# Global attention with its projection in seven block products, and a planner with other costs

## The chip, the cores and the metric

The kernel runs on one core of a Trainium2 chip, as one launch. The metric is the device time of that launch in microseconds (us). Five engines have instruction streams of their own: PE (matrix products into PSUM), DVE (vector work), ACT (activations and copies), POOL (GpSimd) and SP, which here issues nearly all DMAs. All numbers are f32.

## The reference

x has 8 batches of 512 tokens with 256 channels. The result is three residual steps:

```
x = x + 0.5 * ffn(layernorm(x))
x = x + attn(layernorm(x))
x = x + 0.5 * ffn(layernorm(x))
```

ffn is two layers. Each has local attention with 8 heads of 64 (a shift of half the channels by one token; q, k, v from wqkv; q and k normalized, scaled and rotated; a window of 128 keys back; softmax; the projection wo, 512x256) and a gated unit (layernorm, w1 to 2x682, a * gelu(g), w2 back to 256).

attn is the global part, once per batch. With z = layernorm(x), 16 heads of 16 channels, and W_h the h-th 256x256 block of the weight:

```
s_h = softmax(z_h @ z_h.T / 4)       # z_h: 512x16, s_h: 512x512
out = sum over h of s_h @ (z @ W_h)
```

z @ W_h, a 512x256 matrix times a 256x256 one, is the projection that the change is about: 16 heads x 8 batches = 128 times.

## The kernel before

**A recorded program and a planner.** The code doesn't issue instructions. `Recorder` notes each operation as an `Op`, with dependencies from the regions that it reads and writes (`Plan.touch`); `together()` makes one Op, a group, of several products. `Plan.order` then lists all Ops in one order, from which each engine's stream follows: for every engine it knows when the engine is free and when an Op is ready, and takes, among those that can start within 40 ns of the earliest, the one of lowest rank (the order of recording). Durations come from `Plan.cost`: for each Op a time that it keeps its engine and a time until its result is there. For a DMA, `order` adds a pipe of 170 bytes per ns that all DMAs share. These numbers act on the order alone; on the chip each engine runs its list in order and waits for semaphores. `Plan.issue` (line 369) issues everything, so every row of the profile has the line L369, and operations are told apart by tiles.

**Buffers.** `Pool` and `Ring` hand out SBUF slots and the eight PSUM banks. An SBUF tile that is first written from a bank is reserved with the products that fill that bank (line 281), so such a group is placed when a slot is free.

**Streams.** Two local streams, k = 0 and k = 1, take the even and the odd batches. Each goes through eight blocks (four batches, two passes each) of two layers, `attention` (line 566) and `glu` (line 808), and yields between pieces. The first stream runs six pieces ahead (LAG). After each piece of a stream, one piece of the global stream (line 946) is recorded.

**Local attention.** Per tile t of 128 tokens: `front(t)` makes q, k, v; `scores(t)` multiplies q and k and makes the softmax in tiles `p` (two slots per stream, one for each group g of four heads); `values(t)` multiplies by v; `project(t)` applies wo. In `far` blocks (all but the first and the last) p is turned through DRAM by DMAs (`turned_quarters`, `turned_far`), in the other blocks by transposes on PE. wo is kept for both layers, two tiles of 512 KB, loaded at the start with wqkv (line 393).

**Global heads.** Per batch, z is made and transposed into two tiles zT (`gz`), 128 channels x 512 tokens each. `front(h)` (line 965) loads W_h (`wa`) and the head's 16 rows of zT at four offsets (`hT`), and defines three pieces. `scores` makes four 128x512 products and their exponentials (`e`). `project(half)` (line 988) makes two tiles of 128 tokens in one bank, each from two products (the two halves of the channels, accumulated) with 256 moving columns, and copies the bank to `xw` on DVE. `attend(head, t)` (line 1007) multiplies e by xw, and DVE adds the result into x. While one head attends with t = 0 to 3, the next head's scores and two halves are done after t = 0, 1 and 2.

Of the kernel before, what the change touches and what calls it, by code (L numbers as in the profile page):

```python
# [15 lines left out]
P = 128  # L16
B, N, D = 8, 512, 256
NT = N // P
# [158 lines left out]
class Plan:  # L177
# [55 lines left out]
    def cost(self, op):  # L233

        if op.engine == "tensor":

            lanes, op.mode = {}, "whole"
            for name, args, kw in op.calls:
                lane, t = 0, 109.0
                if name == "matmul":  # L240
                    a = kw["lhsT"]
                    lane, t = (a.region()[0], args[0].region()[0]), 2 * max(0.842 * elements(kw["rhs"]), 0.852 * a.shape[1])
                    k, m = a.shape
                    op.mode = "fours" if k <= 32 else "quarters" if k <= 64 and m <= 64 else "halves" if k <= 64 else "columns" if m <= 64 else "whole"
                lanes[lane] = lanes.get(lane, 0.0) + t
            busy = max(lanes.values())
            return busy, busy + 170
        name, args, kw = op.calls[0]
        n = max(elements(a) for a in (*args, *kw.values()) if hasattr(a, "shape"))
        if name == "dma_start":  # L250
            return 580.0, 2300.0
        if op.engine == "scalar":
            if name == "activation":
                op.mode = {AF.Exp: "exp", AF.Gelu: "gelu"}.get(args[2])
                busy = 70 + 0.82 * n + (105 if "bias" in kw else 0)
                return (busy + 93, busy + 310) if "accum_out" in kw else (busy, busy + 110)
            return 70 + 0.81 * n, 175 + 0.81 * n
        if op.engine == "vector":
            if name == "tensor_tensor_reduce":
                return 90.0 + n, 250.0 + n  # L260
            if name == "bn_stats":
                return 70.0 + n, 150.0 + n
            return 90 + 1.035 * n, 170 + 1.035 * n
        if name == "memset":
            return 80 + 0.85 * n, 100 + 0.85 * n
        if ALU.pow in args:
            return 350.0 + 157 * n, 400.0 + 157 * n
        return 210 + 1.98 * n, 250 + 1.98 * n

    def order(self):  # L270

# [18 lines left out]
        pipe = 0.0  # L290
# [17 lines left out]
        while len(order) < len(self.ops):  # L308
# [30 lines left out]
            op.end = op.start + op.done  # L339
            if op.calls[0][0] == "dma_start":  # L340
                a = op.calls[0][2]["out"]
                pipe = max(pipe, op.start + 2000.0) + elements(a) * a.shape[0] * 4 / 170
                op.end = pipe + 300
            for x in op.opens:
                _, x.slot = x.ring.free.pop(0)
                x.ring.open(x.stream, x.turn)
# [29 lines left out]
def macaron(ctx: ExitStack, tc: tile.TileContext, x, weight, wqkv, wo, w1, w2, b2, vecs, qk_scales, rotary, out):  # L376
# [16 lines left out]
    def load_attention(l):  # L393

        wq = wpool.tile([P, 2, 3 * INNER], F32, tag=f"wqkv{l}", name=f"wqkv{l}")
        for part in range(3):
            cols = slice(part * INNER, (part + 1) * INNER)
            nc.sync.dma_start(out=wq[:, :, cols], in_=wqkv[l, :, cols].rearrange("(k p) f -> p k f", p=P))
        o = wpool.tile([P, NPAIR, D], F32, tag=f"wo{l}", name=f"wo{l}")
        nc.sync.dma_start(out=o, in_=wo[l].rearrange("(k p) f -> p k f", p=P))  # L400
        return wq, o

    def load_glu(l):

# [18 lines left out]
    load_x(0)  # L423
    load_x(1)
    attention_weights = [load_attention(0)]
    glu_weights = [load_glu(0)]
    attention_weights.append(load_attention(1))
    tabs, vec = [], []
# [137 lines left out]
    def attention(k, y, l, far):  # L566
        wqkv_sb, wo_sb = attention_weights[l]
# [4 lines left out]
        v = {}  # L572

        kT = work.tile([P, NPAIR, 2, P], F32, tag=f"kT{k}", bufs=1)

# [54 lines left out]
        def scores(t, pair, rn):  # L630
# [21 lines left out]
            for g in range(2):  # L652
# [16 lines left out]
                with plan.together():  # L669
                    for i in range(2):  # L670
                        keys = kT[:, 2 * g + i].rearrange("p j k -> p (j k)")
                        for q, to, ks in sorted(pieces, key=lambda piece: piece[1].start - piece[1].stop):
                            for par in range(2):
                                rows = slice(par * DH, (par + 1) * DH)
                                nc.tensor.matmul(
                                    sps[par][q, i, to], lhsT=qT[rows, 2 * g + i, q], rhs=keys[rows, ks], start=True, stop=True
                                )
                heads = slice(4 * g, 4 * g + 4)

                if far:  # L680
# [51 lines left out]
        def values(t, probs):  # L732
# [63 lines left out]
        for t in range(NT):  # L796
# [128 lines left out]
    def stream(k, blocks):  # L925

        for n, (b, second) in enumerate(blocks):
            while second and (b, True) not in done:
                next(others, None)
            y = layernorm(xs[b], k)  # L930
            yield
            for l in range(DEPTH):
                step = DEPTH * n + l
                far = FAR and 0 < n < len(blocks) - 1
                yield from attention(k, y, l, far)
                yield from glu(k, y, step, xs[b], far)

                if k == 1 and step + 1 < DEPTH * len(blocks):
                    glu_weights.append(load_glu((step + 1) % DEPTH))
                if l == 0 and n + 1 < len(blocks) and blocks[n + 1][0] not in xs:  # L940
                    load_x(blocks[n + 1][0])
            done.add((b, False))
            if second:
                nc.sync.dma_start(out=out[b].rearrange("(t p) c -> p t c", p=P), in_=xs[b])

    def global_heads(b):
# [13 lines left out]
            zT.append(z)  # L960

        def front(h):

            w = work.tile([P, 2, D], F32, tag="wa", bufs=2)
            nc.sync.dma_start(out=w, in_=weight[h * D : (h + 1) * D, :].rearrange("(c p) f -> p c f", p=P))

            hT = work.tile([P, N], F32, tag="hT", bufs=2)  # L970
# [4 lines left out]
            es, xw = [], []  # L975

            def scores():
                sps = [bank([P, N]) for s in range(NT)]
# [4 lines left out]
                for s in range(NT):  # L983
                    e = work.tile([P, N], F32, tag="e", bufs=2 * NT)
                    nc.scalar.activation(e, sps[s], AF.Exp, scale=1.0 / AHD**0.5, accum_out=rsum[:, s : s + 1])
                    es.append(e)

            def project(half):
                pv = bank([P, 2, D])
                with plan.together():  # L990
                    for i in range(2):
                        s = 2 * half + i
                        for c in range(2):
                            nc.tensor.matmul(
                                pv[:, i, :],
                                lhsT=zT[c][:, s * P : (s + 1) * P],
                                rhs=w[:, c, :],
                                start=(c == 0),
                                stop=(c == 1),
                            )  # L1000
                xv = work.tile([P, 2, D], F32, tag="xw", bufs=4)
                nc.vector.tensor_copy(xv, pv)
                xw.append(xv)

            return es, xw, rsum, (scores, lambda: project(0), lambda: project(1))

        def attend(head, t):
            es, xw, rinv, _ = head
            pa = bank([P, D])
            with plan.together():  # L1010
                for s in range(NT):
                    nc.tensor.matmul(
                        pa, lhsT=es[s][:, t * P : (t + 1) * P], rhs=xw[s // 2][:, s % 2, :], start=(s == 0), stop=(s == NT - 1)
                    )
            xt = xs[b][:, t, :]
            nc.vector.scalar_tensor_tensor(xt, pa, rinv[:, t : t + 1], xt, ALU.mult, ALU.add)
# [122 lines left out]
```

## Time and profile before

| | us |
|---|---|
| time, median of 3 runs (3947.79 to 3949.27) | 3949.23 |
| the profiled execution's own time | 3952.0 |
| its span, first to last instruction | 3950.1 |
| PE busy (98% of the span) | 3878.5 |
| PE busy with projection records (work_wa, work_gz), 2048 of them | 477.6 |
| DVE busy (62%) | 2447.9 |
| ACT busy (45%) | 1766.9 |
| POOL busy (31%) | 1233.7 |

A row of a group reads: line, engine, operation, written tile <- read tiles, form (rows x elements), count | busy us, mean ns of one | idle us of the engine before it, and what ended that. In a product's form `128*128 128x256` the first pair is the weights' rows and columns, the second the rows and moving columns. PEld is the loading of weights, which the trace records apart from PE's moving. One f32 product is two records of each. The ends of PE's records are modelled and overlap the next start, so distances from start to start are the safer measure. The granted clock of PE was 0.994 over the whole span.

### The profile page before, as it was taken

To read this page: it belongs to the slowest core of one execution; us is meant where nothing else is said; L and a number is where in the kernel's file an instruction comes from. 1 tells how busy PE (TensorE), PEld (TensorE's weight loads), DVE (VectorE), ACT (ScalarE), POOL (GpSimd) and SP (SyncE) were. 2 spreads that over 40 slices of the span, in tenths; PEclk is the share of its full clock that TensorE was granted. 3 is DMA by queue.
4 is the path that set the end of the run, shared out by engine and by line. 5 is a ranking of instruction groups with operands and counts; after the bars stand their busy time and mean duration, and the time that the engine had idled before them with its cause. 6 is when DMAs were issued, how large, how long until landed. Compare 5 with 4: busy or idle time off the path is not lost.

```text
span 3950.1 us, 72878 instructions
## 1 busy us (share of the span) xinstructions
PE 3878.5 (98%) x26240; PEld 2659.5 (67%) x26240; DVE 2447.9 (62%) x6888; ACT 1766.9 (45%) x4548; POOL 1233.7 (31%) x1132
## 2 busy tenths in 40 slices
PE   8999999999999999999999999999999999999998
PEld 4566776766767667677676776767767667686665
DVE  7676655667566665674765747657466565535674
ACT  5565534535344353452443534535335353324564
POOL 6242323424133341341422405324133242103240
PEclk9999999999999999999999999999999999999999
DMA  3000543534435344253442534525335244110000
GB/s 116 1 24 27 155 135 104 150 98 140 129 104 153 93 128 143 88 165 92 128 138 94 155 104 130 159 91 156 91 116 157 81 143 134 61 33 9 1 24 11
DMA packets 437644, 400.74 MB, mean 101 GB/s; under 512 B 53954, under 2 KB 379172, under 8 KB 437284
## 3 DMA queue, kind: packets, MB, share of 16 engines
q1 hardware_dynamic: 436420, 394.76, 33.5%
q8 instruction: 208, 3.41, 0.4%
q10 hardware_dynamic: 864, 1.33, 0.1%
q14 instruction: 152, 1.25, 0.1%
HBM read 235.49 MB, written 143.66 MB: 96 GB/s over the span
## 4 chain that ended last, share of the span: by engine, by line
PE 81%; DVE 5%; issue 2%; ACT 2%; POOL 1%; DMA 0%; SPq 0%; DVEq 0%; POOLq 0%; ACTq 0%
PE psum_bank L369 81%; ACT work_p L369 2%; DVE work_p L369 2%; DVE work_qn L369 1%; DVE small_ss L369 1%; POOL small_rn L369 0%; POOL work_t L369 0%; ACT work_both L369 0%; DVE work_xw L369 0%; DVE small_bnst L369 0%; SPq L369 0%; DVE work_both L369 0%; DVE work_o L369 0%; DVE xpool_x L369 0%; POOL small_rstd L369 0%
## 5 line engine op out<-in xcount | busy, mean ns | idle before, releaser
L369 PE MATMUL psum_bank<-work_xw,work_e 128*128 128x256 f32 x4096 | 960.0, 385 | 3.0 <-ACT work_e L369 1.9
L369 PEld LDWEIGHTS psum_bank<-work_xw,work_e 128*128 128x128 f32 x4096 | 765.8, 191 | 199.0 <-issue 47.2
L369 PE MATMUL psum_bank<-wpool_wqkv,zpool_z 128*128 128x512 f32 x1536 | 712.2, 603 | 2.7 <-ACT work_v L369 2.0
L369 ACT ACTIVATE work_p<-work_p,small_nmax,small_rn 128x192 f32<-128x192 f32 (+2 forms) x1024 | 543.7, 533 | 324.2 <-DVE small_nmax L369 213.7
L369 POOL TENSOR_TENSOR work_t<-work_qn,const_tab 128x256 f32<-128x256 f32 x512 | 397.4, 797 | 590.3 <-ACT work_qn L369 503.5
L369 PE MATMUL psum_bank<-zpool_z,wpool_w 128*128 128x512 f32 x1280 | 558.9, 595 | 1.5 <-DVE zpool_z L369 1.5
L369 POOL TENSOR_TENSOR small_rn<-small_ss,const_nhalf 128x8 f32<-128x8 f32 x256 | 484.4, 1893 | 149.8 <-DVE small_ss L369 141.6
L369 POOL TENSOR_TENSOR work_p<-work_p,small_ri 128x768 f32<-128x768 f32 (+1 forms) x192 | 264.4, 1378 | 778.9 <-DVE small_ri L369 371.9
L369 ACT ACTIVATE work_e<-psum_bank 128x512 f32<-128x512 f32 x512 | 298.3, 596 | 420.4 <-PE psum_bank L369 403.9
L369 PE MATMUL psum_bank<-work_wa,work_gz 128*128 128x256 f32 x2048 | 477.6, 381 | 5.9 <-DVE work_gz L369 3.9
L369 PEld LDWEIGHTS psum_bank<-wpool_wqkv,zpool_z 128*128 128x128 f32 x1536 | 284.8, 192 | 288.1 <-issue 266.4
L369 PEld LDWEIGHTS psum_bank<-zpool_z,wpool_w 128*128 128x128 f32 x1280 | 243.5, 191 | 301.8 <-issue 273.7
L369 PEld LDWEIGHTS psum_bank<-work_wa,work_gz 128*128 128x128 f32 x2048 | 385.3, 190 | 78.3 <-issue 14.7
L369 DVE SCALAR_TENSOR_TENSOR xpool_x<-psum_bank,gsmall_rinv,xpool_x 128x256 f32<-128x256 f32 x512 | 242.2, 474 | 283.6 <-PE psum_bank L369 281.2
L369 ACT COPY work_qn<-psum_bank 128x512 f32<-128x512 f32 x256 | 148.4, 582 | 327.1 <-PE psum_bank L369 263.8
L369 DVE SCALAR_TENSOR_TENSOR work_p<-psum_bank,const_vec,work_p 128x512 f32<-128x512 f32 x128 | 95.7, 749 | 278.1 <-PE psum_bank L369 226.9
L369 PE MATMUL psum_bank<-wpool_wo,work_o 128*128 128x256 f32 x1024 | 244.9, 383 | 6.4 <-DVE work_o L369 6.2
L369 PE MATMUL psum_bank<-wpool_w,work_p 128*128 128x256 f32 x1024 | 243.2, 380 | 0.0
L369 DVE COPY work_xw<-psum_bank 128x512 f32<-128x512 f32 x256 | 173.8, 680 | 108.4 <-PE psum_bank L369 107.9
L369 DVE TENSOR_REDUCE small_ss<-work_sq 128x8 f32<-128x512 f32 x256 | 172.2, 673 | 109.0 <-ACT work_sq L369 108.1
L369 PEld LDWEIGHTS psum_bank<-wpool_wo,work_o 128*128 128x128 f32 x1024 | 191.4, 190 | 56.7 <-DVE work_o L369 16.1
L369 ACT ACTIVATE work_p<-psum_bank,const_vec 128x512 f32<-128x512 f32 x128 | 87.9, 687 | 296.6 <-PE psum_bank L369 288.0
(89 smaller groups left out, 4943.3 us busy)
## 6 DMA issues: line engine op xcount, KB each, us to landing
work_p<-dram_quarters SPq DMA_DIRECT2D x576, 128.0 KB
dram_quarters<-work_p SPq DMA_DIRECT2D x288, 192.0 KB
dram_turned<-work_both SPq DMA_DIRECT2D x96, 512.0 KB
work_both<-dram_turned SPq DMA_DIRECT2D x384, 128.0 KB
work_wa<-in_weight_dram SPq DMA_DIRECT2D x128, 256.0 KB
wpool_w<-in_w_dram SPq DMA_DIRECT2D x48, 640.0 KB
work_hT<-work_gz SPq DMA_DIRECT2D x512, 32.0 KB
dram_turned<-work_p SPq DMA_DIRECT2D x48, 256.0 KB
```

The lines of the kernel that those rows point to most:

```text
L369: getattr(getattr(nc, op.engine), name)(*map(real, args), **{k: real(a) for k, a in kw.items()})
```

## The change

It has four parts.

**The projection.** z is split into four blocks of 256 tokens x 128 channels (a11, a12, a21, a22, views of zT), W_h into four of 128x128 (b11 to b22). POOL makes four sums of the a's once per batch (tile `sums`) and four differences of the b's per head, three instructions. Seven products of blocks take the place of eight: each is two products on PE with 128 moving columns, one per tile of tokens. They lie in four groups, with a bank each: a11 b11; a12 b21 and s2 t2; s3 t3 and s1 t1; a22 t4 and s4 b22. An ACT copy (`u1`) and four additions on DVE put the blocks of the result together in `xw`, in place of two copies. `attend` reads the same elements of xw, in another layout. hT has one buffer in place of two.

**wo per layer.** One tile, loaded at the start and then again for every layer step, recorded where the second stream ends its attention (15 more times).

**The planner's numbers.** DMAs, ACT, DVE and POOL get other constants, with terms for PSUM sources and for operands that are single values per partition; the shared DMA pipe is 330 bytes per ns in place of 170; SP isn't given a further DMA while eight are under way by the plan.

**Scores behind the last values.** In far blocks the score groups of a tile t > 0 get a dependency on both value groups of the tile before.

```diff
         if name == "dma_start":
-            return 580.0, 2300.0
+            source = kw["in_"]
+            far = isinstance(source, View) and source.tile.ring.space == DRAM
+            return (560.0 if len(source.shape) > 3 and far else 450.0), 2400.0 if far else 1900.0
         if op.engine == "scalar":
+            base = 60 if args[1].tile.ring.space == PSUM else 100
...
-                busy = 70 + 0.82 * n + (105 if "bias" in kw else 0)
-                return (busy + 93, busy + 310) if "accum_out" in kw else (busy, busy + 110)
-            return 70 + 0.81 * n, 175 + 0.81 * n
+                busy = base + 0.82 * n + (105 if "bias" in kw else 0)
+                return (busy + 92, busy + 280) if "accum_out" in kw else (busy, busy + 105)
+            return base + 0.81 * n, base + 105 + 0.81 * n
         if op.engine == "vector":
...
-            return 90 + 1.035 * n, 170 + 1.035 * n
+            pointers = sum(isinstance(u, View) and elements(u) == 1 for u in args[1:])
+            busy = 70 + 1.035 * n + (55 if pointers and name == "scalar_tensor_tensor" else 27 * pointers)
+            return busy, busy + 85
...
         if ALU.pow in args:
-            return 350.0 + 157 * n, 400.0 + 157 * n
-        return 210 + 1.98 * n, 250 + 1.98 * n
+            return 248.0 * n - 10, 248.0 * n + 30
+        busy = 140 + (2.14 if n <= 2 * P else 1.67) * n
+        return busy, busy + 45
...
-                pipe = max(pipe, op.start + 2000.0) + elements(a) * a.shape[0] * 4 / 170
-                op.end = pipe + 300
+                pipe = max(pipe, op.start + op.done - 400) + elements(a) * a.shape[0] * 4 / 330
+                op.end = pipe + 400
+                flying = sorted(flying + [op.end])[-8:]
+                if len(flying) == 8:
+                    free[e] = max(free[e], flying[0])
...
+                if far and t > 0:
+                    plan.ops[-1].after.update(latest)
...
+                    latest[g:] = [plan.ops[-1]]
...
+        if k == 1 and step + 1 < 2 * DEPTH * B // 2:
+            output_weights.append(load_wo((step + 1) % DEPTH))
...
+        a11, a12, a21, a22 = (zT[c][:, r * N // 2 : (r + 1) * N // 2] for r in range(2) for c in range(2))
+        sums = work.tile([P, 4, N // 2], F32, tag="sums")
+        for i, (u, v, op) in enumerate(
+            ((a21, a22, ALU.add), (sums[:, 0], a11, ALU.subtract), (a11, a21, ALU.subtract), (a12, sums[:, 1], ALU.subtract))
+        ):
+            nc.gpsimd.tensor_tensor(sums[:, i], u, v, op)
+        s1, s2, s3, s4 = (sums[:, i] for i in range(4))
...
+            nc.gpsimd.tensor_tensor(diffs[:, :2], blocks[:, 1::2], blocks[:, :2], ALU.subtract)
+            t1, t3, t2, t4 = (diffs[:, i] for i in range(4))
+            nc.gpsimd.tensor_tensor(t2, b22, t1, ALU.subtract)
+            nc.gpsimd.tensor_tensor(t4, b21, t2, ALU.subtract)
...
+            def product(*pairs):
+                ps = bank([P, len(pairs), 2, P])
+                with plan.together():
+                    for i, (left, right) in enumerate(pairs):
+                        for t in range(2):
+                            nc.tensor.matmul(ps[:, i, t, :], lhsT=left[:, t * P : (t + 1) * P], rhs=right, start=True, stop=True)
+                return ps.rearrange("p i t f -> p i (t f)")
+
             def project(half):
-                pv = bank([P, 2, D])
-                with plan.together():
-                    for i in range(2):
-                        s = 2 * half + i
-                        for c in range(2):
-                            nc.tensor.matmul(
-                                pv[:, i, :], lhsT=zT[c][:, s * P : (s + 1) * P], rhs=w[:, c, :], start=(c == 0), stop=(c == 1),
-                            )
-                xv = work.tile([P, 2, D], F32, tag="xw", bufs=4)
-                nc.vector.tensor_copy(xv, pv)
-                xw.append(xv)
+                spread = lambda u: u.unsqueeze(1).to_broadcast([P, 2, N // 2])
+                pairs = whole.rearrange("p (a b) m -> p b a m", b=2)
+                if half == 0:
+                    p1 = product((a11, b11))
+                    u1 = work.tile([P, N // 2], F32, tag="u1")
+                    nc.scalar.copy(u1, p1[:, 0])
+                    nc.vector.tensor_add(pairs[:, 0], product((a12, b21), (s2, t2)), spread(u1))
+                    return
+                ps = product((s3, t3), (s1, t1))
+                nc.vector.tensor_add(pairs[:, 1], ps, spread(whole[:, 2]))
+                nc.vector.tensor_add(whole[:, 2], ps[:, 1], whole[:, 1])
+                nc.vector.tensor_add(pairs[:, 1], product((a22, t4), (s4, b22)), pairs[:, 1])
```

`whole` is `xw` as four blocks of 256 columns, each two token tiles of 128 channels.

More of the change, by code (lines that the diff above doesn't have):

```diff
@@ L250, in cost @@
         if name == "dma_start":
-            return 580.0, 2300.0
+            source = kw["in_"]
+            far = isinstance(source, View) and source.tile.ring.space == DRAM
+            return (560.0 if len(source.shape) > 3 and far else 450.0), 2400.0 if far else 1900.0
         if op.engine == "scalar":
+            base = 60 if args[1].tile.ring.space == PSUM else 100
             if name == "activation":
                 op.mode = {AF.Exp: "exp", AF.Gelu: "gelu"}.get(args[2])
-                busy = 70 + 0.82 * n + (105 if "bias" in kw else 0)
-                return (busy + 93, busy + 310) if "accum_out" in kw else (busy, busy + 110)
-            return 70 + 0.81 * n, 175 + 0.81 * n
+                busy = base + 0.82 * n + (105 if "bias" in kw else 0)
+                return (busy + 92, busy + 280) if "accum_out" in kw else (busy, busy + 105)
+            return base + 0.81 * n, base + 105 + 0.81 * n
         if op.engine == "vector":
             if name == "tensor_tensor_reduce":
-                return 90.0 + n, 250.0 + n
+                return 86.0 + n, 190.0 + n
             if name == "bn_stats":
-                return 70.0 + n, 150.0 + n
-            return 90 + 1.035 * n, 170 + 1.035 * n
+                return 60.0 + n, 145.0 + n
+            pointers = sum(isinstance(u, View) and elements(u) == 1 for u in args[1:])
+            busy = 70 + 1.035 * n + (55 if pointers and name == "scalar_tensor_tensor" else 27 * pointers)
+            return busy, busy + 85
         if name == "memset":
@@ L289, in order @@
         free, mode = dict.fromkeys(self.ENGINES, 0.0), dict.fromkeys(self.ENGINES)
-        pipe = 0.0
+        pipe, flying = 0.0, []
         candidates = {e: [op for op in self.ops if op.engine == e and not op.waits] for e in self.ENGINES}
@@ L398, in load_attention, with load_wo @@
             nc.sync.dma_start(out=wq[:, :, cols], in_=wqkv[l, :, cols].rearrange("(k p) f -> p k f", p=P))
-        o = wpool.tile([P, NPAIR, D], F32, tag=f"wo{l}", name=f"wo{l}")
+        return wq
+    def load_wo(l):
+        o = wpool.tile([P, NPAIR, D], F32, tag="wo")
         nc.sync.dma_start(out=o, in_=wo[l].rearrange("(k p) f -> p k f", p=P))
-        return wq, o
+        return o
     def load_glu(l):
@@ L425, in macaron @@
     attention_weights = [load_attention(0)]
+    output_weights = [load_wo(0)]
     glu_weights = [load_glu(0)]
@@ L564, in later, with attention @@
         return later_of[k]
-    def attention(k, y, l, far):
-        wqkv_sb, wo_sb = attention_weights[l]
+    def attention(k, y, step, far):
+        l = step % DEPTH
+        wqkv_sb, wo_sb = attention_weights[l], output_weights[step]
         z0 = zpool.tile([P, N + 1], F32, tag=f"z{k}", bufs=2)
@@ L571, in attention @@
         z1 = shifted(tiled, k)
-        v = {}
+        v, latest = {}, []
         kT = work.tile([P, NPAIR, 2, P], F32, tag=f"kT{k}", bufs=1)
@@ L934, in stream @@
                 far = FAR and 0 < n < len(blocks) - 1
-                yield from attention(k, y, l, far)
+                yield from attention(k, y, step, far)
                 yield from glu(k, y, step, xs[b], far)
@@ L960, in global_heads @@
             zT.append(z)
-        def front(h):
-            w = work.tile([P, 2, D], F32, tag="wa", bufs=2)
-            nc.sync.dma_start(out=w, in_=weight[h * D : (h + 1) * D, :].rearrange("(c p) f -> p c f", p=P))
-            hT = work.tile([P, N], F32, tag="hT", bufs=2)
+        a11, a12, a21, a22 = (zT[c][:, r * N // 2 : (r + 1) * N // 2] for r in range(2) for c in range(2))
[5 more added lines that the diff above has]
+        s1, s2, s3, s4 = (sums[:, i] for i in range(4))
+        def front(h):
+            w = work.tile([P, 2, 4, P], F32, tag="wa", bufs=2)
+            blocks, diffs = w[:, 0], w[:, 1]
+            nc.sync.dma_start(
+                out=blocks.rearrange("p (c f) q -> p c (f q)", c=2),
+                in_=weight[h * D : (h + 1) * D, :].rearrange("(c p) f -> p c f", p=P),
+            )
+            b11, b12, b21, b22 = (blocks[:, i] for i in range(4))
+            nc.gpsimd.tensor_tensor(diffs[:, :2], blocks[:, 1::2], blocks[:, :2], ALU.subtract)
+            t1, t3, t2, t4 = (diffs[:, i] for i in range(4))
+            nc.gpsimd.tensor_tensor(t2, b22, t1, ALU.subtract)
+            nc.gpsimd.tensor_tensor(t4, b21, t2, ALU.subtract)
+            hT = work.tile([P, N], F32, tag="hT", bufs=1)
             at = h % (P // AHD) * AHD
@@ L974, in front @@
             rsum = gsmall.tile([P, NT], F32, tag="rsum")
-            es, xw = [], []
+            es = []
+            xw = work.tile([P, 4, 2, P], F32, tag="xw", bufs=2)
+            whole = xw.rearrange("p i t f -> p i (t f)")
             def scores():
@@ L986, in scores @@
                     es.append(e)
-            def project(half):
-                pv = bank([P, 2, D])
-                with plan.together():
-                    for i in range(2):
-                        s = 2 * half + i
-                        for c in range(2):
-                            nc.tensor.matmul(
[L995 to L999, printed above, removed]
-                            )
-                xv = work.tile([P, 2, D], F32, tag="xw", bufs=4)
-                nc.vector.tensor_copy(xv, pv)
-                xw.append(xv)
+            def product(*pairs):
[5 more added lines that the diff above has]
+                return ps.rearrange("p i t f -> p i (t f)")
+            def project(half):
+                spread = lambda u: u.unsqueeze(1).to_broadcast([P, 2, N // 2])
[10 more added lines that the diff above has]
+                nc.vector.tensor_add(pairs[:, 1], product((a22, t4), (s4, b22)), pairs[:, 1])
             return es, xw, rsum, (scores, lambda: project(0), lambda: project(1))
@@ L1012, in attend @@
                     nc.tensor.matmul(
-                        pa, lhsT=es[s][:, t * P : (t + 1) * P], rhs=xw[s // 2][:, s % 2, :], start=(s == 0), stop=(s == NT - 1)
+                        pa.rearrange("p (i f) -> p i f", i=2),
+                        lhsT=es[s][:, t * P : (t + 1) * P],
+                        rhs=xw[:, (slice(0, 4, 3), slice(1, 3))[s // 2], s % 2, :],
+                        start=(s == 0),
+                        stop=(s == NT - 1),
                     )
```

## The prediction

> **What bounds the kernel now.** I read the page's busy shares and slices first, then the busy times of stretches, then PE's timeline, then the groups of the other engines. From the page:
>
> ```profile
> span 3950.1 us, 72878 instructions
> ...
> PE 3878.5 (98%) x26240; PEld 2659.5 (67%) x26240; DVE 2447.9 (62%) x6888; ACT 1766.9 (45%) x4548; POOL 1233.7 (31%) x1132
> ...
> PE   8999999999999999999999999999999999999998
> ```
>
> Busy times by stretch (length; busy time and instructions of each engine; granted clock; DMA share; GB/s):
>
> ```profile
> 0.00:100.00 100.00, 80.40 (x632) 47.84 (x633) 79.03 (x225) 56.65 (x147) 63.32 (x73) 1.00 0.34 115
> 100.00:300.00 200.00, 189.67 (x1510) 119.97 (x1509) 137.18 (x396) 117.55 (x281) 66.39 (x64) 0.98 0.04 12
> 300.00:3300.00 3000.00, 2985.89 (x20089) 2063.33 (x20088) 1883.34 (x5314) 1312.52 (x3459) 976.03 (x873) 1.00 0.41 122
> 3300.00:3600.00 300.00, 298.07 (x1585) 222.15 (x1584) 126.78 (x323) 83.81 (x231) 28.72 (x28) 1.00 0.19 55
> 3800.00:3950.00 150.00, 131.84 (x994) 84.17 (x992) 86.09 (x250) 77.98 (x169) 29.12 (x27) 0.94 0.02 8
> ```
>
> From 300 to 3600 us, where the global heads run beside the local layers, PE idles 16 of 3300 us. The other 56 us of its 71.6 us of idle lie at the two ends, without heads. In the middle all other work fills in behind PE: a microsecond taken off PE's queue there is a microsecond off the end, and work added to DVE, ACT or POOL costs nothing until PE waits for it.
>
> **Seven products (project).** Before, a head has 8 products with 256 moving columns; the trace has 2048 records for 128 x 8 = 1024 calls, so two records per product, each with its weight load. After, it has 14 products with 128 moving columns: 28 records of 128x128. No such f32 product is in the trace, so its price is bounded. PE's timeline:
>
> ```profile
> 355.23 1.89 PE L369 MATMUL psum_bank<-work_wa,work_gz 128*128 128x256 f32 x8
> 356.96 0.82 PE L369 MATMUL psum_bank<-const_ident,work_p 128*128 128x128 f32 x6
> 357.62 1.89 PE L369 MATMUL psum_bank<-work_wa,work_gz 128*128 128x256 f32 x8
> 359.35 3.60 PE L369 MATMUL psum_bank<-zpool_z,wpool_w 128*128 128x512 f32 x8
> ```
>
> Ends are modelled, so I go from start to start: 8 records of 256 columns take 1.73 us (216 ns each), 6 transposes with 128 columns and 128x128 weights of their own 0.66 us (110 ns each). The danger is the weight load: its record lasts 190 ns (page, mean), and if it couldn't run ahead, 28 x 0.190 = 5.32 us would replace 2 x 1.73 = 3.46 us. So 110 ns below, 190 ns above. Two rows of f32 products that are not transposes decide, in another window:
>
> ```profile
> 2004.27 0.31 PEld L369 LDWEIGHTS psum_bank<-work_hT 16*128 16x128 f32 x8 [0.33 <-issue]
> ...
> 2009.54 0.90 PE L369 MATMUL psum_bank<-work_p,work_v 64*64 64x128 f32 x32
> ...
> 2010.37 1.99 PE L369 MATMUL psum_bank<-work_xw,work_e 128*128 128x256 f32 x8
> ```
>
> Eight loads of 128 columns, two on each of four sets of 16 rows, end within 0.31 us although each lasts 0.18: the second follows the first by at most 0.13 us. And the 32 records of values are eight rounds of four at a time, 128 and 64 columns in turn, each with a load of 64 columns. At 110/128 = 0.86 ns per column moving takes 4 x 192 x 0.86 = 0.66 us, the loads 8 x 55 = 0.44 us; one after the other would be 1.10 us, and the group took 0.83. Loads as long as what they hide behind are hidden. I take 110 ns: 28 x 0.110 = 3.08 us per head, 0.38 us less, **-49 us** over 128 heads.
>
> [...]
>
> **Twice as many groups.** Two groups of products per head become four, each with its own bank, so 256 more entries. An entry is free in the rows above (1.73 us for 8 both times) and costs about 0.09 us where work of another kind comes next (from 2002.45, where eight of the same records start, to 2004.27 is 1.82 us). Bounds 0 and 256 x 0.09 = 23 us. Entries between neighbouring products are near the free row; I take a quarter, **+6 us**.
>
> **DVE, ACT and POOL.** Prices of the added operations, from groups by form:
>
> ```profile
> L369 DVE COPY work_xw<-psum_bank 128x512 f32<-128x512 f32 x256 | 173.8, 680 | 108.4 <-PE psum_bank L369 107.9
> ...
> L369 DVE TENSOR_TENSOR work_o<-psum_bank,work_o 128x512 f32<-128x512 f32 x96 | 65.6, 683 | 24.4 <-ACT work_o L369 23.8
> ...
> L369 ACT COPY work_both<-psum_bank 128x256 f32<-128x256 f32 x32 | 10.6, 369 | 10.6 <-PE psum_bank L369 10.6
> L369 DVE TENSOR_TENSOR work_o<-psum_bank,work_o 128x256 f32<-128x256 f32 x32 | 13.3, 416 | 1.5 <-ACT work_o L369 1.5
> ...
> L369 POOL TENSOR_TENSOR const_tab<-const_tab,zpool_z 128x256 f32<-128x256 f32 x8 | 5.7, 741 | 3.2 <-DMA zpool_z<-in_qk_scales_dram 3.2
> ```
>
> DVE: two copies of 680 ns go, three additions of 683 and one of 416 come: 2465 - 1360 = +1.1 us per head, 141 us; it rises from 63% to 67% in the middle. ACT: one copy of 369, 47 us, 45% to 46%. POOL: per head one subtraction of 256 columns (741 ns) and two of 128, which the trace lacks (between half of 741 and 741; I take 500): 1.74 us, 223 us, and four of 741 per batch, 24 us: about 250 us, 31% to 38%. All lies under PE's 2986 of 3000 us and I cost it at nothing; bare, DVE's part would be 141 us. One piece can show. The last half was one copy behind the last product. Now the third group needs 0.68 + 0.42 = 1.1 us of DVE while the fourth occupies PE for 8 x 0.110 = 0.88, so the last addition starts 0.22 us late, on every head 28 us. PE already waits here:
>
> ```profile
> PEld psum_bank L369 <- DVE work_xw L369: 26.2, 35, 1.3
> ```
>
> 35 waits for 256 copies, 14%; as PE mostly has other work in between, I charge about that share, **+3 us**.
>
> [...]
>
> **wo per layer.** 16 loads of 512 KB in place of 2, 7 MB more beside 401 MB; 14 more issues of 0.37 us on SP. With one buffer a load waits for the second stream's last projection and has to land by the first stream's next one. Between these the trace has some 70 us (groups at 603 and 674, 345 and 421 us), and 512 KB at the 122 GB/s of the middle are 4 us: 0. On SP the load stands ahead of the round trips through DRAM of both streams; planned behind the projection it waits for, it holds them only if PE lags the plan. The single buffer of hT likewise gets a head's length (11.6 us at the least: 160 records in ten heads from 3480 to 3596 us) for four loads of 32 KB: 0.
>
> **Planner and scores.** New costs and at most eight DMAs in flight move every engine's order, without altering a single instruction; scores of a later tile of a far block now stand behind both value groups of the tile before, whose p buffers they mostly need anyway. No row prices an order. Below: all of PE's idle time, -71 us. Above: PE idling in the middle as it does from 100 to 300 us (5.2% in place of 0.5%), 3300 x 4.7% = +155 us. I take 0, as the middle's 16 us are nearer to nothing left to gain and the filling work hasn't shrunk.
>
> **Sum.** -49 + 6 + 3 = -40 us. The profiled execution took 3952.0 us (span 3950.1 and 1.9 around it), 2.8 over the median of 3949.2; it becomes 3912, the median **3909 us**, -1.0%.
>
> **Rivals.** *The new order also fills the ends* (chance 0.12): half of the 56 us of idle at the ends goes with the 40: 3880. For it: the ends have gaps that a truer model can see. Against: they lie where streams wait for their own chain. *Entries and waits eat the gain* (0.06): 23 us of entries and 15 us of waits for xw in place of 6 and 3 leave -11 us, and a few more none: 3945. *The new order starves PE* (0.12, the slower one): the planner now lets DMAs land earlier (330 bytes per ns in place of 170), so DVE, ACT and POOL queues can stand behind a tile of p still under way, and PE behind them. It decides from 40 us: PE idle in the middle at 0.5 + 40/3300 = 1.7%. At 2.5%, +66 us, it gives 3975. For it: SP already waits in order; against: heads are ready to fill nearly any gap. I count loads that don't hide within this 0.12. That the products don't fall in time at all is this last case.
>
> **How the numbers follow.** The forecast holds 0.70, with its own range 3885 to 3935 (entries and waits at their ends, the order at +-15). A measurement tells 0.2%, 8 us, from no change. Faster: 0.70 + 0.12 = 0.82; same 0.06; slower 0.12. The range runs from 3872, where the first rival is nearly covered, to 3946, which leaves out the slower case.
>
> **What would show it.** 3584 records of 128x128 for work_gz, 110 ns from start to start; PE busy near 3840 us; ten heads in the lone stretch near the end in 112 us in place of 116; DVE near 2590 us, POOL near 1485. Wrong would be: starts 124 ns apart or more, PE idle over 1.7% in the middle, or weight loads waiting for xw well over 26 us.

## The result

The changed kernel takes **4067.6 us** (median of 5 runs, 4062.6 to 4081.3), against 3949.2 us before: **1.0308 times as long, 95% interval 1.0288 to 1.0328**, 118 us more. Forecast were 3909 us, with a range from 3872 to 3946.

### The profile page after: what moved, and what is told of

Same layout as the page of the kernel before. It is cut to its first block, busy times and chain, and to the rows that moved or that the text cites. A ratio compares the mean times of both kernels' runs of the same rounds, so it can differ in the third digit from the quotient of the medians.

```text
span 4070.3 us, 77051 instructions
## 1 busy us (share of the span) xinstructions
PE 3902.9 (96%) x27776; PEld 2740.7 (67%) x27776; DVE 2583.0 (63%) x7144; ACT 1821.5 (45%) x4690; POOL 1464.4 (36%) x1548
## 5 line engine op out<-in xcount | busy, mean ns | idle before, releaser
L381 PE MATMUL psum_bank<-work_xw,work_e 128*128 128x256 f32 x4096 | 981.0, 388 | 21.4 <-DVE work_xw L381 10.0
L381 POOL TENSOR_TENSOR work_t<-work_qn,const_tab 128x256 f32<-128x256 f32 x512 | 386.9, 776 | 507.6 <-ACT work_qn L381 501.1
L381 POOL TENSOR_TENSOR work_wa<-work_wa 128x128 f32<-128x128 f32 (+1 forms) x384 | 220.4, 576 | 721.8 <-DMA work_wa<-in_weight_dram 576.0
L381 PE MATMUL psum_bank<-work_wa,work_sums 128*128 128x128 f32 x2048 | 294.5, 277 | 3.7 <-POOL work_sums L381 2.9
L381 PEld LDWEIGHTS psum_bank<-work_wa,work_sums 128*128 128x128 f32 x2048 | 269.4, 193 | 18.2 <-issue 4.8
L381 DVE TENSOR_TENSOR work_xw<-psum_bank,work_xw 128x512 f32<-128x512 f32 (+1 forms) x384 | 228.2, 594 | 55.0 <-PE psum_bank L381 45.5
```

The costliest lines, as they stand in the source:

```text
L381: getattr(getattr(nc, op.engine), name)(*map(real, args), **{k: real(a) for k, a in kw.items()})
```

## The profile after

The page of the changed kernel: span, busy shares, and PE by slices.

```profile
span 4070.3 us, 77051 instructions
...
PE 3902.9 (96%) x27776; PEld 2740.7 (67%) x27776; DVE 2583.0 (63%) x7144; ACT 1821.5 (45%) x4690; POOL 1464.4 (36%) x1548
...
PE   8999999999999999999999999999999999999998
```

Its busy times by stretch, with the same columns as before:

```profile
100.00:300.00 200.00, 186.69 (x1512) 119.69 (x1505) 134.65 (x396) 120.76 (x285) 66.19 (x62) 0.98 0.05 15
300.00:3300.00 3000.00, 2907.57 (x20522) 2056.64 (x20521) 1924.86 (x5319) 1320.06 (x3429) 1116.84 (x1179) 0.98 0.40 120
```

DVE and POOL came out as forecast (2590 and 1485 us). What is new is PE's idle time, 167 us in place of 72, and of the 96 us more, 78 lie in the middle stretch (92 of 3000 us in place of 14). PE's busy time didn't fall to 3840; it rose by 24, and the granted clock of the middle stretch is 0.98 where it was 1.00. The slices hide this: 97% is still a 9.

Who PE waited for, the longest and two more (us in total, times, longest):

```profile
PE psum_bank L381 <- DMA work_p<-dram_quarters: 44.1, 47, 2.6
...
PE psum_bank L381 <- DVE work_xw L381: 12.8, 16, 1.8
...
PE psum_bank L381 <- DMA work_p<-dram_turned: 2.6, 3, 1.9
```

Before, PE waited for no DMA of p at all, and 1.4 us in all for xw (`PE psum_bank L369 <- DVE work_xw L369: 1.4, 3, 0.7`). Now it stops 47 times at a value group whose p is still on its way back from DRAM. One of these stops in PE's timeline (start, length from first start to last end):

```profile
2074.24 1.05 PE L381 MATMUL psum_bank<-work_wa,work_sums 128*128 128x128 f32 x8
2075.14 0.61 PE L381 MATMUL psum_bank<-work_wa,work_gz 128*128 128x128 f32 x4
...
2079.19 1.11 PE L381 MATMUL psum_bank<-work_p,work_v 64*64 64x128 f32 x36
2082.94 1.54 PE L381 MATMUL psum_bank<-work_p,work_v 64*64 64x128 f32 x28 [2.65 <-DMA work_p<-dram_quarters]
2084.41 3.78 PE L381 MATMUL psum_bank<-work_xw,work_e 128*128 128x256 f32 x8
2087.99 2.39 PE L381 MATMUL psum_bank<-wpool_wo,work_o 128*128 128x256 f32 x8
```

Two things are to be seen. The forecast price of the new products holds: 8 records of 128 columns take 0.90 us (2074.24 to 2075.14), 112 ns each. And after the 2.65 us of waiting, the next 8 records of 256 columns take 3.58 us (2084.41 to 2087.99), 447 ns each in place of 216. The busy times around this place, with the granted clock as the third number from the end, say why:

```profile
2068.00:2082.00 14.00, 12.29 (x110) 10.40 (x108) 11.90 (x35) 3.17 (x10) 3.10 (x3) 1.00 0.63 188
2082.20:2089.00 6.80, 6.06 (x39) 5.08 (x40) 1.18 (x2) 1.35 (x3) 1.63 (x3) 0.50 0.69 229
2089.00:2103.00 14.00, 14.00 (x56) 8.46 (x55) 4.58 (x11) 5.45 (x12) 0.00 (x0) 1.00 0.16 43
```

This wait cost twice: its own length of 2.65 us, and then time at half clock. The clock falls 1.9 us after PE ran out of work and stays at half for 6.8 us, of which PE works 6.1. Not every wait does this: the middle stretch of this trace has 39 stops of PE of over 0.9 us, and at 21 of them such a dip begins during the stop or within 4 us behind it. Over the span the mean clock is

```profile
core 0: 4070.3 us, clock 0.982
```

```profile
core 0: 3950.1 us, clock 0.994
```

after and before. Added up from the records of the clock, 145 us of 4070 are at half speed in place of 46 of 3950; less the 11.5 and 4.0 us in which PE stood still anyway, 133 and 42 us are left, and half the difference, by this estimate about 46 us, is lost (447 ns a record above in place of 216). That the stops bring the dips is read from where they lie in time. Over the runs below, half-speed time grows with PE's idle time, but not in step: 56 us with 118 idle in before_latency, 104 with 137 in before_newcosts.

## The experiments

All compare with the kernel before, run again beside them on the same chip (medians 3946 to 3947 us); proj_wo, the projection with only what it needs in memory, serves as a base for others. Each diff shows what the label changes in its base.

### Which part loses: proj_wo, before_newcosts, after_olddma, before_signal

proj_wo is the change without the planner's numbers and without the dependency of scores. (wo per layer and the single buffer of hT stay with it.)

```diff
-            return (560.0 if len(source.shape) > 3 and far else 450.0), 2400.0 if far else 1900.0
+            return 580.0, 2300.0
...
-                pipe = max(pipe, op.start + op.done - 400) + elements(a) * a.shape[0] * 4 / 330
-                op.end = pipe + 400
+                pipe = max(pipe, op.start + 2000.0) + elements(a) * a.shape[0] * 4 / 170
+                op.end = pipe + 300
```

after_olddma is the changed kernel with just these lines taken back and the limit in flight left out; proj_wo takes back the other costs and the dependency too. before_newcosts puts all new numbers into the kernel before. before_signal has `SIGNAL = 112.0` in place of 110, the planner's allowance for a semaphore: the same work in a slightly other order.

> The kernel before with the seven-product projection and wo per layer, but the planner's old numbers and no dependency of scores on the last values. Theory A (the new DMA numbers make the order too early, PE then waits for the quarters of p): 3905 to 3930 us, PE waits for DMA work_p<-dram_quarters under 5 us. Theory B (the projection's own work on DVE, POOL and the banks starves PE whatever the order): 4030 to 4080 us.

> The kernel before with only the planner's new numbers (all engines, the DMA pipe and the limit of eight in flight). Theory A: 4000 to 4080 us, with PE waiting 40 us or more for DMA work_p<-dram_quarters. Theory B: within 15 us of the kernel before, 3935 to 3965 us.

> The changed kernel with only the DMA numbers of the planner put back (580 and 2300 ns, a pipe of 170 bytes per ns, no limit in flight); ACT, DVE and POOL keep the new ones. Theory A: 3905 to 3935 us, PE hardly waits for DMAs. Theory B: 4040 to 4080 us. If the new numbers of the engines are to blame and not those of the DMAs: 4000 to 4070 us.

> The kernel before with the planner's allowance for a semaphore at 112 ns in place of 110: the same work, another order. It measures what any new order moves by itself. Theories A and B: within 10 us of 3949. Theory C (every order but the one found is worse by chance): 3980 us or more.

| run | us | ratio, 95% interval |
|---|---|---|
| proj_wo | 3965.0 | 1.0045 (1.0030 to 1.0059) |
| before_newcosts | 4040.5 | 1.0231 (1.0214 to 1.0248) |
| after_olddma | 3965.5 | 1.0047 (1.0032 to 1.0062) |
| before_signal | 3948.9 | 1.0004 (0.9995 to 1.0012) |

The planner's numbers, which change no instruction, lose 94 us by themselves, and the DMA numbers are 102 of the 118 us. Theory A holds in its first half: the DMA numbers lose the time. But no theory foresaw 3965 us for proj_wo and after_olddma, where A asked for 3930 or 3935 at most: the projection gains nothing without the new numbers; it loses 18 us.

### The DMA numbers: before_latency, after_p90

before_latency has the new landing times and pipe, without a limit in flight and with the old costs of the engines. after_p90 is the changed kernel with later landings alone:

```diff
-            return (560.0 if len(source.shape) > 3 and far else 450.0), 2400.0 if far else 1900.0
+            return (560.0 if len(source.shape) > 3 and far else 450.0), 3900.0 if far else 2900.0
```

> The kernel before with the planner's new DMA latencies and the pipe of 330 bytes per ns, but no limit of eight in flight; costs of ACT, DVE and POOL old. Theory A1 (the plan takes transfers to be there too early): 4020 to 4050 us, PE waits 40 us or more for DMA work_p<-dram_quarters. Theory A2 (the limit in flight moves the DMAs' order, and that is what costs): within 10 us of the kernel before.

> The changed kernel with only the planner's time to a DMA's landing raised, from 2400 and 1900 ns to 3900 and 2900, near the late tenth of the landings that other engines waited for in the changed kernel's trace; the pipe of 330 bytes per ns and all else stay. Theory A (planned landings at the middle of the trace are too early for engines that run in order): 3955 to 3985 us, as with the old DMA numbers. If only the slow pipe of 170 helps, as it spaces transfers out: 4030 to 4060 us.

before_latency: 3999.1 us, 1.0129 (1.0113 to 1.0145). after_p90: **3959.9 us**, 1.0026 (1.0015 to 1.0038), 108 us below the changed kernel. The wait for the quarters of p, in before_latency and then in after_p90:

```profile
PE psum_bank L371 <- DMA work_p<-dram_quarters: 29.8, 38, 2.2
```

```profile
PE psum_bank L381 <- DMA work_p<-dram_quarters: 2.5, 6, 0.8
```

So the cause is when the plan takes a transfer to have landed: put later, it ends the loss, though the pipe stays fast. before_latency and before_p90 (below), which differ in the landing times alone and have no limit in flight, are 44 us apart in the same way; before_latency itself falls short of the 4020 us and the 40 us of waiting that theory A1 asked for. In the change, though, the constant for a read back from DRAM didn't get shorter: with its surcharge it rose from 2300 to 2400 ns. What brought the landings forward was the pipe, 0.40 us for 128 KB in place of 0.77, with hardly a queue behind it. Worked out with each kernel's own planner, the 576 reads of quarters are planned to land this long after their issue:

| planner of | middle, us | ninetieth percentile, us |
|---|---|---|
| before | 4.6 | 7.6 |
| the changed kernel | 2.8 | 2.8 |
| after_p90 | 4.3 | 4.3 |

In the changed kernel's trace, the reads of quarters that some engine waited for landed 2.96 us after their issue in the middle and 3.9 us at the ninetieth percentile (77 of them; those that nobody waited for leave no time). 60 of the 77 landed later than the planned 2.8 us, 4 later than 4.3. A value group needs the last of several transfers, and PE takes its list in order (the attend products of 2084.41 above stood behind the stop, though every xw written before them was there by 2080.63), so there was no slack for the late ones. The old pipe of 170 bytes per ns is slower than what the chip moved in the stretch above (229 GB/s), so it was wrong, and it left slack. No run changes the pipe's rate alone.

### The engines' numbers and the dependency: before_engines, after_nobehind

before_engines has the new costs of ACT, DVE and POOL with the DMA lines old; after_nobehind is

```diff
-                if far and t > 0:
-                    plan.ops[-1].after.update(latest)
```

> The kernel before with the planner's new numbers for ACT, DVE and POOL alone, the DMA numbers old. With the DMA latencies alone it took 3999 us, with all new numbers 4040. If the engines' numbers cost by themselves: 3985 to 3995 us. If they cost only where the plan has no slack left for the DMAs: 3942 to 3956 us.

> The changed kernel without the dependency of scores on the last values. If that dependency costs nothing, as forecast: 4055 to 4080 us. If it holds PE's freedom to fill gaps and so is part of the loss: 4020 to 4045 us. If it shortens the waits for the quarters, and without it they grow: 4085 us or more.

before_engines: 3972.7 us, 1.0068 (1.0053 to 1.0083): between the two expectations, PE idle 88 us in place of 72. With them and the limit in flight, the DMA numbers make 4040 in place of 3999 (before_newcosts against before_latency); no run has the limit alone, which by the planner holds SP back 32 times in before_newcosts. On top of the seven products the engines' numbers and the dependency cost nothing that shows (after_olddma against proj_wo). Why they cost here isn't settled. after_nobehind: 4060.0 us, 1.0286 (1.0270 to 1.0303), so the dependency costs at most some 8 us and is no part of the story.

### Why the projection doesn't gain: before_wo_hT, proj_nodiff, proj_copies

before_wo_hT is the kernel before with wo per layer and `hT` at `bufs=1`. The other two are proj_wo with part of the work left out:

```diff
-            nc.gpsimd.tensor_tensor(diffs[:, :2], blocks[:, 1::2], blocks[:, :2], ALU.subtract)
-            t1, t3, t2, t4 = (diffs[:, i] for i in range(4))
-            nc.gpsimd.tensor_tensor(t2, b22, t1, ALU.subtract)
-            nc.gpsimd.tensor_tensor(t4, b21, t2, ALU.subtract)
+            t1, t3, t2, t4 = b11, b12, b21, b22
```

```diff
-                    nc.scalar.copy(u1, p1[:, 0])
-                    nc.vector.tensor_add(pairs[:, 0], product((a12, b21), (s2, t2)), spread(u1))
+                    nc.vector.tensor_copy(pairs[:, 0], product((a12, b21), (s2, t2)))
...
-                nc.vector.tensor_add(pairs[:, 1], ps, spread(whole[:, 2]))
-                nc.vector.tensor_add(whole[:, 2], ps[:, 1], whole[:, 1])
-                nc.vector.tensor_add(pairs[:, 1], product((a22, t4), (s4, b22)), pairs[:, 1])
+                nc.vector.tensor_copy(pairs[:, 1], product((a22, t4), (s4, b22)))
```

> The kernel before with wo loaded per layer step into one tile and one buffer for hT; the projection in eight products, the planner old. If these two cost nothing: within 8 us of the kernel before, 3940 to 3957 us. If SP's queue or the single buffers hold the streams, and that is why the seven products gained nothing: 3980 to 4010 us.

> proj_wo (3965 us) with the per-head differences on POOL left out, the blocks of W standing in their place, so the result is not that of the projection. Theory P (POOL's queue, which stops at a subtraction until wa has landed, delays what stands behind it): 3905 to 3925 us. If POOL is covered, as forecast: 3958 to 3968 us.

> proj_wo (3965 us) with the ACT copy and the four DVE additions replaced by two copies of 512 columns, so the products aren't added up. Theory D (DVE's added 1.1 us per head and its longer chain starve PE): 3905 to 3930 us. If DVE is covered, as forecast: 3955 to 3968 us. If four groups and banks per head are to blame, neither this run nor the one without differences comes below 3950 us.

before_wo_hT: 3955.3 us, 1.0022 (1.0015 to 1.0029), so the single buffers and the 14 more loads cost 8 to 9 us, just past the 8 us allowed for nothing. proj_nodiff: 3964.3 us, 1.0041 (1.0027 to 1.0055); POOL is covered, as forecast, though its queue waits 347 us for wa in proj_wo. proj_copies: 3959.3 us, 1.0033 (1.0021 to 1.0044), 6 less than proj_wo; DVE's additions are a small part. No single suspect holds the missing gain. PE's idle time says the same: 107 us in proj_wo, 108 in proj_copies, 100 in proj_nodiff, in place of 72. In proj_wo 33 of the 36 us more lie in the middle stretch, and three of the waits are much longer than before (in proj_wo, then before, where PE had no sums to wait for):

```profile
300.00:3300.00 3000.00, 2953.12 (x21192) 2085.68 (x21192) 1990.82 (x5498) 1384.90 (x3578) 1167.90 (x1221) 0.99 0.41 123
PE psum_bank L369 <- DVE work_o L369: 15.2, 16, 3.0
PE psum_bank L369 <- DVE work_xw L369: 14.7, 15, 2.6
PE psum_bank L369 <- POOL work_sums L369: 5.4, 6, 1.5
```

```profile
PE psum_bank L369 <- DVE work_o L369: 6.2, 9, 1.4
```

### The price of the form and of the groups: before_split, before_four

before_split cuts each of the eight products into two of 128 columns, in the same two groups; before_four puts the eight into four groups and banks, each with a copy of its own.

```diff
+                        for f in range(2):
+                            cols = slice(f * P, (f + 1) * P)
...
-                                pv[:, i, :],
...
+                                    pv[:, i, cols],
...
+                                    rhs=w[:, c, cols],
```

```diff
-                pv = bank([P, 2, D])
...
+                for i in range(2):
+                    pv = bank([P, D])
...
+                    nc.vector.tensor_copy(xv[:, i], pv)
```

> The kernel before with every product of the projection cut into two of 128 moving columns: 32 records of 128 in place of 16 of 256, in the same two groups per head, all else as it was. It measures the price of the form alone. If a record costs 112 ns, as in the changed kernel: 128 x (32 x 0.112 - 16 x 0.216) = +16 us, 3958 to 3968 us, projection rows 473 us from start to start. If the short form also loses time at each entry, or stops weight loads from running ahead: 3975 us or more. If it is free: 3947.

> The kernel before with the projection's eight products in four groups and banks per head in place of two, each with a copy of 256 columns: the same records on PE, twice the groups. Theory E (entries of groups and their banks cost near 0.09 us each and more in stalls): 3970 to 3990 us. If entries are nearly free, as forecast: 3947 to 3957 us.

before_split: 3976.9 us, 1.0080 (1.0065 to 1.0095); before_four: 3960.7 us, 1.0036 (1.0022 to 1.0051). Both miss the expectation of small prices; before_split lies in the range of its second branch, before_four between its two. I added up, in each trace, the time from the start of every projection record to the start of PE's next record:

| | records | bare, at 216 or 112 ns | added up, us | over bare |
|---|---|---|---|---|
| before | 2048 of 256 | 442 | 456 | 14 |
| before_four | 2048 of 256 | 442 | 469 | 26 |
| before_split | 4096 of 128 | 459 | 477 | 18 |
| proj_wo | 3584 of 128 | 401 | 444 | 42 |

Twice the groups is 12 us on PE (47 ns an entry), the form 4 us more than its bare price. (before_split loses 31 us in all, so 10 of them lie elsewhere.) In proj_wo both come together with waits, and of 41 us of bare gain 13 are left.

### Is it the order: before_sig140, proj_sig140, proj_entry

`SIGNAL = 140.0` in the kernel before and in proj_wo; and proj_wo with PE's costs nearer to the trace:

```diff
-                    lane, t = (a.region()[0], args[0].region()[0]), 2 * max(0.842 * elements(kw["rhs"]), 0.852 * a.shape[1])
+                    lane, t = (a.region()[0], args[0].region()[0]), 2 * max(0.842 * elements(kw["rhs"]), 0.875 * a.shape[1] if a.shape[1] == elements(kw["rhs"]) == P else 0.852 * a.shape[1])
...
-            busy = max(lanes.values())
+            busy = max(lanes.values()) + 45
```

> The kernel before with the planner's allowance for a semaphore at 140 ns in place of 110: the same work in an order that differs more than at 112. Theory C (the order of before is a lucky one, and any that differs clearly loses 10 to 30 us): 3957 to 3980 us. If orders are much alike: 3940 to 3955 us.

> proj_wo (3965 us) with the semaphore allowance at 140 ns. Theory C (the order of proj_wo is an ordinary one, and the products' own gain of 10 to 15 us on PE is there below it): 3940 to 3980 us, below before_sig140 or equal to it within 15 us. If the seven products lose by themselves: above before_sig140 by 15 us or more.

> proj_wo (3965 us) with the planner told what the trace shows of PE: 112 ns a record of 128x128, and 45 ns more for every group. If the plan's blindness to these holds the gain back: 3915 to 3945 us. If not: 3955 to 3980 us, within the scatter of orders.

before_sig140: 3951.6 us, 1.0012 (1.0005 to 1.0018); proj_sig140: 3993.5 us, 1.0117 (1.0102 to 1.0132); proj_entry: 4036.3 us, 1.0222 (1.0205 to 1.0239). Two other orders of the kernel before (SIGNAL at 112 and 140) lie within 5 us of it, so theory C, a lucky order of before, isn't borne out. With seven products the same step moves the time by 28 us, to 42 above before_sig140, as if the products lost by themselves (proj_p90 below says otherwise); and a truer cost of PE makes it 71 us worse, a plain miss: a planner's numbers that are each nearer to the trace needn't give a better order. Why PE starves in that one (154 us idle) stays open.

### Late landings with and without the projection: before_p90, proj_p90

The kernel before and proj_wo with the landings of after_p90 and the pipe of 330 bytes per ns.

> The kernel before with landings planned late: 3900 and 2900 ns and the pipe of 330 bytes per ns, without a limit in flight; costs of ACT, DVE and POOL old. Beside before_latency (3999 us) it differs in the landing times alone. Theory A: 3935 to 3960 us, no wait of PE for the quarters of p. Below 3939 us it beats both kernels.

> proj_wo (3965 us) with the same late landings as before_p90. If the seven products lose by their own waits (PE for work_xw), it stands 10 to 30 us above before_p90, with 10 us or more of PE idle on work_xw. If what they lost in proj_wo was the old pipe's order: at or below before_p90, 3905 to 3940 us.

before_p90: 3955.1 us, 1.0017 (1.0009 to 1.0025). proj_p90: **3945.8 us**, 1.0003 (0.9994 to 1.0013), the best version with seven products, level with the kernel before and 9 us below before_p90. So the first expectation holds for the wait for xw alone, the second for the place below before_p90, but not for its range. before_p90 is in its range, but PE still waits 12.4 us for the quarters, which late landings were to end. What stayed of the products' cost is the wait for xw. In proj_p90, then in before_p90:

```profile
PE psum_bank L371 <- DVE work_xw L371: 14.9, 16, 1.6
```

```profile
PE psum_bank L371 <- DVE work_xw L371: 1.4, 1, 1.4
```

It is 12 to 22 us in every kernel with the seven products and their additions, 0.7 to 3.8 in every one with eight, and 5.4 in proj_copies. This wait belongs to the change. Nothing run here beats both kernels beyond the measurement.

## Why the prediction was wrong

**The step that failed first is "Planner and scores", where I took 0.** Its upper bound, +155 us, and the third rival, the order that starves PE, held what happened, with the mechanism nearly as told: a faster pipe lets transfers land too early in the plan. It expected the queues of DVE, ACT and POOL to stand, and PE behind them; in the trace it is PE itself that stands at the quarters of p (44 us). The planner's own end even fell, from 3898 to 3855 us, while the kernel's rose. I weighed it by the middle's 16 idle us, "nearer to nothing left to gain". That speaks about what a new order could win, and says nothing about what it could lose. The row that would have decided was not read: how long after its issue a transfer is there. In the trace of before, the 19 reads of quarters that an engine waited for landed 2.76 us after issue in the middle and 3.7 at the ninetieth percentile; the old plan had 4.6 us in the middle, the new one has 2.8. Of the 118 us, 108 go with the landing times alone (after_p90, in whose plan the limit in flight also holds SP back 261 times in place of 22).

**The rival's price was too small.** At 3.1% of idle in the middle, its own rule would have given 3300 x 2.6% - 40 = +46 us. It left out the clock: about 46 us more, since about half of the stops of over 0.9 us in the middle stretch (21 of 39) came with 3.4 to 10.2 us at half speed. With this the span nearly closes: of its 120 us more, 96 are idle time of PE, and of the 24 us more of busy time -41 are the shorter records, +12 the entries of groups and +46 the clock, 17 together. In the trace the granted clock has two values, 0.50 and 1.00; it fell 1.9 us into the stop of 2.65 us above, and at shorter stops too, as 0.6 us into one of 1.69 us (at 1876.8).

**Seven products, -49: the price was right, the gain wasn't.** A record costs 112 ns, not 110 (+7 us), and stays under the 124 at which 28 of them take the 3.46 us of the 16 before. Where heads run alone near the end the gain is there nearly whole, 0.3 of 0.32 us: POOL's timeline of proj_wo shows one head per 11.3 us, against 11.6 before.

```profile
3507.95 1.79 POOL L369 TENSOR_TENSOR work_wa<-work_wa 128x256 f32<-128x256 f32 x3 [9.44 <-DMA work_wa<-in_weight_dram]
3519.23 1.79 POOL L369 TENSOR_TENSOR work_wa<-work_wa 128x256 f32<-128x256 f32 x3 [9.49 <-DMA work_wa<-in_weight_dram]
3530.56 1.79 POOL L369 TENSOR_TENSOR work_wa<-work_wa 128x256 f32<-128x256 f32 x3 [9.54 <-DMA work_wa<-in_weight_dram]
```

Beside the local streams it isn't. The wait for xw was read from the weight loads' row (26.2 us in before), while PE itself waited 1.4 us for it; and 14% of 28 us is nearer to 4 than to the 3 charged. Proj_wo against the forecast of -40:

| step | forecast, us | measured, us |
|---|---|---|
| bare records | -49 | -41 |
| entries of groups | +6 | +12 (before_four) |
| xw late | +3 | +13 (1.4 to 14.7, idle of PE) |
| wo and hT | 0 | +8 to 9 (before_wo_hT) |
| form beyond its price, other waits | 0 | the rest, some +25 |
| sum | -40 | +18 |

The terms were each taken in another kernel, so the last row is a remainder and not a measurement. Within the profiled executions of before and proj_wo the account is direct: PE's busy time fell by 23 us (3855.2 in place of 3878.5), and its idle time rose by 36. Of these, 13 are at xw, 9 at work_o and 5 at the sums. What brings them, and the rest, stays open; leaving out the additions or the differences doesn't end them. That the loss varies with the order (+18, +42, -9 us against the same planner with eight products) suggests that much of it is lost through order: a head has more pieces, and PE stops at more of them (116 stops of over 0.15 us in place of 78).

**wo, at nothing:** wrong by 8 to 9 us together with hT, which the search for slack between two uses of wo couldn't see. **POOL and DVE's sums, at nothing:** right within 6 us (proj_nodiff, proj_copies), but for the 5 us in which PE waits for the sums of a batch. **The dependency of scores:** right within 8 us.

## What to carry to other kernels

- For an order that in-order engines will follow, a planned landing at the middle of the trace was too early here. Numbers near the late tenth won back 108 us in the changed kernel and 44 of 53 us in the kernel before, with no instruction changed.
- A matrix engine at 98% with hardly any idle time bounds what a new order can win, not what it can lose: price a new plan from both sides, and give the loss its chance.
- Fewer operations that come in more dependent pieces can lose their gain where other work competes: here they won 0.3 us per head alone, while the whole kernel went from 42 us lost to 9 won, by the order. Measure the gain in the mixed stretch too.

## What the runs showed of the hardware that was not expected

Short stops of PE can come with a fall of its clock: in the changed kernel one of 2.65 us saw 6.8 us at a granted clock of 0.50, in which 256 moving columns took 447 ns in place of 216. The dips in this trace and in that of before last 3.4, 6.8 or 10.2 us, but for the last, which the end of the trace cuts. Over the span, 145 us in place of 46 were at half speed. An f32 product with 128 moving columns and weights of its own costs 112 ns a record, 4% over half of one with 256.
